# Layer 0's value convolution of images 1 to 7: from halves once to halves twice, with tokens still on partitions

## The chip, the cores and the metric

The kernel runs on one core of a Trainium2 chip. The metric is the device time of one execution in microseconds (us); lower is better. Every time of one engine's work below comes from a single execution recorded by the hardware profiler.

## The reference, cut to what matters

Eight images of 512 channels and 32 x 32 = 1024 tokens, all in float32, pass through two attention blocks. A 1x1 convolution is a matrix product of a 512 x 512 weight with the 512 x 1024 image.

```python
# layer 0: 8 heads of 64 channels, 32 norm groups
h = group_norm(x)                                  # over groups of 16 channels
q, k, v = split(w_qkv @ h + b_qkv)                 # three 512 x 512 products
weight = softmax((q * s)^T (k * s))                # per head, 1024 x 1024
a = v weight^T                                     # per head
x = x + w_proj @ a + b_proj

# layer 1: one head of 512 channels, 8 norm groups
xn = group_norm(x); q, k, v = q_w xn + q_b, k_w xn + k_b, v_w xn + v_b
x = x + p_w @ (softmax(q^T k / sqrt(512)) v) + p_b
```

## The kernel before, in words

**Products by halves.** The 512-wide products are done with the seven-product scheme of Strassen and Winograd. In a "once halved" product (`by_token`, `by_channel`, `values1`) both factors are cut in halves in both directions and seven products of half the size replace eight. In a "twice halved" product (`conv2`, line 498) each of the seven products is cut again in the same way, so 49 products of 128 x 128 weights replace 64. What such a product needs ahead of TensorE's work: sums of quarters of the weight, made once in the prologue and kept in DRAM (`keep` at line 290 for once halved, `keep2` at 296 for twice halved, which computes four further sums on GpSimd at line 306); sums of halves of the normed image, the *image factors* `t_h` (`image_factors`, on VectorE); and for twice halved products the *inner factors* `inner_h` (`inner_factors`, 28 subtractions on GpSimd at line 411 for an image). The sums of the results run on the engines that empty PSUM: VectorE and ScalarE, and GpSimd at line 532 for a few.

**Which product has which form, before.** Layer 0's v and layer 1's z (the folded value and projection weights) are once halved with tokens on partitions: the image is the stationary factor and the weights move, 256 columns at a time. Layer 0's k and q and layer 1's g (image times m, the folded key and query weights) are twice halved with channels on partitions: the weights are stationary, the image moves, 256 columns at a time. The projection p is once halved, channels on partitions. In `conv2` a pair of outer products runs seven steps j; `ps` has a 256-column half for each of the pair's products:

```python
def mm(ps, j, start):
    for i, p in enumerate(products):
        matmul(ps[:, i, :], w[:, i, j - 1, :], f[p][j], start=..., stop=True, skip_group_check=True)
```

Every matmul of the program appears as two records in the trace, on TensorE's matmul row (PE) as on its weight-load row (PEld). All of them come from one helper, line 67, so groups are told apart by the names of their tiles: `psa_v`, `psb_v` and `psc_v` are the PSUM tiles of v, and so on.

**Order of the work.** The first image's v, q and k are made in the prologue, once halved. Then for each image b the main loop does: layer 0's attention of image b (`attention0`); its projection with the residual, and a store to DRAM (`projection`, line 927); layer 1 of image b - 1 (g, scores, z, and the weighted sum `values1`, whose tiles are called `av`, with the output's stores at line 750); then v, k and q of image b + 1 (`values`, `keys_and_queries`). Image 0 has no layer 1 before it, so it goes from attention to v of image 1, then to its own projection, then k and q. One period of the loop, from image to image, is about 348 us.

**Queues.** TensorE's order is that of the program. A product's last two steps (3 and 4 of its last pair) are deferred and run behind step 1 of the next product, so that TensorE has work while PSUM is emptied. Work of the other engines is hung in as *hooks* after a given step, or as a `background` list of which a step takes one or more entries; the image factors, the inner factors and the norm statistics of the next image are such entries. VectorE, ScalarE, GpSimd and SyncE, which issues the DMAs, each take their queue in order; a scheduler orders what isn't pinned with `tc.keep_in_program_order`.

**Buffers.** Images and factors live in a rotating pool of 32 tiles of 128 x 1024 elements (`big_tile`). Weights come from DRAM in the order of the list `uses` into a pool of three buffers of 1792 KB (`wpool`, tag "w"); `load_weight` (lines 325 and 328) issues the next load of that list when a product has taken its weights. The norm statistics of image b + 1 are made from a load of their own, called `ahead`, during v of image b; the image itself is loaded again, as `h`, when it is normed, in the weighted sum of layer 1 (`begun`, line 209).

Of the kernel before, what the change touches and what calls it, by code (L numbers as in the profile page):

```python
# [9 lines left out]
F32 = mybir.dt.float32  # L10
# [19 lines left out]
def two_attention_blocks_kernel(  # L30
# [145 lines left out]
    def main_path(ctx):  # L176
# [114 lines left out]
            nc.sync.dma_start(wdram[n], t)  # L291


        wdram2 = {n: dram.tile([P, 7, 7, P], F32, name=f"sums2_{n}") for n in "qkm"}

        def keep2(n, t):

            u = wpool.tile([P, 4, 7, P], F32, tag="w", name=f"prepare2_{n}")
            quarter = lambda k, i: t[:, :, k, ts(i, P)]
            a11, a21, a12, a22 = quarter(0, 0), quarter(0, 1), quarter(1, 0), quarter(1, 1)  # L300
            s1, s2, s3, s4 = (u[:, i, :, :] for i in range(4))
            for dst, x, y, op in (
                (s1, a21, a22, ALU.add), (s2, s1, a11, ALU.subtract), (s3, a11, a21, ALU.subtract),
                (s4, a12, s2, ALU.subtract),
            ):
                tc.keep_in_program_order(nc.gpsimd.tensor_tensor(dst, x, y, op))
            for j, f in enumerate((a11, a12, s4, a22, s1, s2, s3)):
                nc.sync.dma_start(wdram2[n][:, :, j, :], f)

        twice = {n: [(n, 0), (n, 1)] for n in wdram2}  # L310
        uses = ["v", "p", *twice["k"], *twice["q"]] if B > 1 else ["p"]
        for b in range(1, B):
            uses += ["p", *twice["m"], "z"] + (["v", *twice["k"], *twice["q"]] if b + 1 < B else [])
        uses += [*twice["m"], "z"]
        loaded = []

# [178 lines left out]
            tail.extend([lambda: step(3), lambda: step(4)])  # L495
            tail.extend(final)

        def conv2(n, f, bias, name, hooks=(), after=()):

            out = channel_tiles(name)
            hooks = list(hooks)

            def blocks(places, r, cc):

                if len(places) == 2 and places[0][0] == places[1][0] and places[0][1] < places[1][1]:
                    t = out[2 * places[0][0] + r].rearrange("p (c q n) -> p c q n", c=2, q=2)  # L510
                    return [t[:, :, cc, :]]
                return [
                    out[2 * i + r].rearrange("p (c q n) -> p c q n", c=2, q=2)[:, c : c + 1, cc, :] for i, c in places
                ]

            def add(dst, ps, x):

                n = max(len(dst), len(x))
                for i in range(n):
                    d = dst[i] if len(dst) == n else dst[0][:, i : i + 1, :]  # L520
                    psi = ps[:, i : i + 1, :] if n > 1 else ps
                    xi = x[i] if len(x) == n else x[0][:, i : i + 1, :]
                    if isinstance(d, tuple):
                        d, oc = d
                        nc.vector.scalar_tensor_tensor(d, psi, bias[:, oc : oc + 1], xi, ALU.add, ALU.add)
                    else:
                        nc.vector.tensor_add(d, psi, xi)  # L527

            def more(dst, x, y, r, cc):

                (d,), (x,), (y,) = (blocks([at], r, cc) for at in (dst, x, y))
                nc.gpsimd.tensor_tensor(d, x, y, ALU.add)  # L532

            def biased_half(i, c):
                if bias is not None:
                    for r in range(2):
                        oc = 2 * i + r
                        t = out[oc][:, ts(c, HT)]
                        tc.keep_in_program_order(nc.scalar.activation(t, t, AF.Identity, bias=bias[:, oc : oc + 1]))

            def pair(s, products, y, x, final):
                def written(r, cc):
                    to = blocks(y, r, cc)
                    if s < 3 or bias is None:
                        return to
                    return [(t, 2 * i + r) for t, (i, _) in zip(to, y)]

                w = weights2[s // 2][:, (0, 2, 0, 1)[s] :]

                def mm(ps, j, start):  # L550
                    for i, p in enumerate(products):
                        matmul(ps[:, i, :], w[:, i, j - 1, :], f[p][j], start=start and i == 0, stop=True, skip_group_check=True)

                def extra(r, cc, read, done):
                    if products == (7,):
                        if read:
                            more((0, 1), (0, 1), (1, 1), r, cc)
                        if done:
                            more((1, 1), (1, 0), (1, 1), r, cc)

                inner_steps(
                    f"{name}_{s}", s % 2, len(products), mm, add, written, x and (lambda *at: blocks(x, *at)),
                    extra, hooks.pop(0) if hooks else (), final,
                )

            weights2 = [weight_part((n, 0))]
            pair(0, (1, 5), [(1, 0), (1, 1)], None, [])
            pair(1, (2, 6), [(0, 0), (0, 1)], [(1, 0), (1, 0)], [load_weight, lambda: biased_half(0, 0)])
            weights2.append(weight_part((n, 1)))
            pair(2, (7,), [(1, 0)], [(0, 1)], [lambda: biased_half(1, 1)])  # L570
            pair(3, (3, 4), [(0, 1), (1, 0)], [(0, 1), (1, 0)], [load_weight, *after])
            return out
# [31 lines left out]
        def attention0(b, q, k, v, a, extra):  # L604
            n = 0

            for hp in range(KC):
                for tb in (0, 1) if hp < KC - 1 else (1, 0):
# [22 lines left out]
                    for s in range(NS):  # L631
                        for j in range(2):
                            matmul(
                                av[ts(j, 64), :], v[s // 2][:, s % 2, hp * P + j * 64 : hp * P + (j + 1) * 64],
                                es[s][:, j, :], start=(s == 0), stop=(s == NS - 1),
                            )
                    for f in extra.pop(0) if extra else ():
# [175 lines left out]
        def prologue():  # L813
# [26 lines left out]
            v = by_token(weight_factors(first["v"][0]), hf, "v0_0", middle=(2, 5, 6, 7), back=4)  # L840
            finish()
            run_background(len(background))
            keep("v", first["v"][0])
            x1 = [load_x(1, c, "x1") for c in range(KC)] if B > 1 else []
            norm1 = GroupNorm(0, "0_1")
            background.extend(lambda c=c: norm1.stats(c, x1[c]) for c in range(len(x1)))
# [21 lines left out]
                lambda: tc.keep_in_program_order(nc.vector.tensor_add(obias[0], bias[2], pcols("bp0"))),  # L868
                load_weight,
            ])  # L870
            return v, q, k, norm1, later

        psum_pools("first", 2)
        v, q, k, norm0, later = prologue()
# [11 lines left out]
        def begun(load, norm, b, what):  # L886
# [3 lines left out]
            def start(c):  # L890
# [3 lines left out]
                t, [lambda c=c: start(c) for c in range(KC)],  # L894
                [lambda c=c: norm.apply(nc.scalar, t[c], t[c], c) for c in range(KC)],
            )

        def projection(b, af, xt, hooks=()):

# [39 lines left out]
                [lambda: norm.affine(acc_tile(f"gvar_{uid}")[:, :KC])],  # L939
            ]  # L940

        def values(b, hf, hooks=()):

            inner, steps = inner_factors(hf, f"h0_{b}")
            background.extend(steps)
            norm = None
            if b + 1 < B:
                norm = GroupNorm(0, f"0_{b + 1}")
                for c in range(KC):
                    background.append(lambda c=c: norm.stats(c, load_x(b + 1, c, "ahead")))  # L950
            v = by_token(weight("v"), hf, f"v0_{b}", middle=(2, 5, 6, 7), hooks=hooks, back=4, after=[load_weight])
            return v, inner, norm

        def keys_and_queries(b, f, norm, hooks):

# [45 lines left out]
        for b in range(B):  # L1001
# [21 lines left out]
                    extra[2 * i + 3] += fs  # L1023
            elif B > 1:
                hf, t = image_factors(h, "h0_1", here)
                for i, fs in enumerate((t[:2], (t[2], t[4]), (t[6], t[3]), (t[5], t[7]))):
                    extra[2 * i + 7] += fs
            psum_pools(f"attention_{b}", 1)
            scaled = attention0(b, q, k, v, a, extra)
            if b > 0:  # L1030
                for f in steps[4:7]:
                    f()
            psum_pools(f"products_{b}", 2)
            xt = [load_x(b, c, "x") for c in range(KC)]
            if b > 0:

                inner, sums2 = inner_factors(hf, f"h1_{b - 1}", tc.keep_in_program_order)
                for f in sums2:
                    f()
                norm1, stats = projection(b, af, xt, [scaled, steps[7]])  # L1040
                gf, gsteps = layer1_scores(b - 1, inner)
                _, _, mean, affine = norm_hooks(norm1, f"1_{b}")
                if b + 1 < B:
                    h, loads, applies = begun(load_x, norm0, b + 1, "h0")
                else:
                    h, loads, applies = begun(load_again, norm1, b, "h1")
                ahead = [loads, *([f] for f in applies)]
                layer1_rest(b - 1, inner, gf, gsteps, stats, [[], mean, [], affine], ahead)
                if b + 1 < B:
                    hf, steps = image_factors(h, f"h0_{b + 1}")  # L1050
                    background.extend(steps)
                    v, f, norm0 = values(b + 1, hf)
                    q, k = keys_and_queries(b + 1, f, norm0, ())
            elif B > 1:
                v, f, norm0 = values(1, hf, [[], [], [], [], [*steps[:7], scaled, steps[7]]])
                norm1, stats = projection(0, af, xt)
                hooks = norm_hooks(norm1, "1_0")
                hooks[0].append(lambda: background.extend(stats))
                q, k = keys_and_queries(1, f, norm0, hooks)
            else:  # L1060
                for f in (*steps[:7], scaled, steps[7]):
                    f()
# [211 lines left out]
```

## Time and profile before

| what | value |
|---|---|
| median of 3 runs | 2842.77 us (2842.6 to 2843.14) |
| span of the profiled execution | 2841.1 us |
| what lies around the span, from the median | 1.7 us |
| TensorE busy, and its granted clock | 99%, full speed |
| VectorE, GpSimd, ScalarE busy | 73%, 42%, 33% |
| DMA | 280.6 MB, 98 GB/s |
| records on TensorE's matmul row | 11,846 |

The span runs from the first instruction to the last, and the metric is a little longer. The busy shares are averages over stages of a different kind, so each stage is read by itself. The stages that the change touches lie as follows for image 2, in us from the span's start: the weighted sum `av` of layer 1 from 554.96, its last steps ending at 613.5; v with its first step at 596.3 and the rest from 613.5 to 635; k to 656.9; q to 677.8; layer 0's attention to 795. In image 0's case, attention ends at 237.6, v of image 1 runs to 265.4, the projection to 286.6, and k and q to 330.2.

```profile
core 0: us, PE busy (x) PEld busy (x) DVE busy (x) ACT busy (x) POOL busy (x), PEclk, DMA share, GB/s
554.50:613.50 59.00, 59.00 (x169) 30.61 (x169) 41.23 (x51) 7.28 (x8) 33.60 (x36) 1.00 0.35 132
613.50:635.00 21.50, 21.50 (x101) 18.84 (x100) 13.03 (x24) 1.74 (x3) 0.00 (x0) 1.00 0.35 119
635.00:656.90 21.90, 21.90 (x104) 18.90 (x103) 12.69 (x34) 4.41 (x8) 7.03 (x11) 1.00 0.42 148
656.90:677.80 20.90, 20.84 (x95) 17.52 (x94) 12.83 (x31) 6.67 (x11) 5.88 (x10) 1.00 0.73 277
677.80:795.00 117.20, 117.20 (x574) 42.91 (x576) 98.71 (x85) 68.13 (x76) 20.55 (x14) 1.00 0.13 46
```

Each row is a stretch of time with the busy time of each engine in it and the number of its records; DVE is VectorE, ACT ScalarE, POOL GpSimd, PE TensorE.

### The profile page before, as it was taken

The numbers are of one execution on the slowest core, as the hardware profiler recorded it, in microseconds if no ns is written. First come the engines' busy times: TensorE is split into PE (matmuls) and PEld (weight loads), VectorE is DVE, ScalarE is ACT, GpSimd is POOL, SyncE is SP. The second block draws the span as 40 slices with busy tenths as digits, with TensorE's granted clock in tenths as the row PEclk, the third lists the DMA queues.
The fourth block names the chain that finished last, engine by engine and source line by source line (L and its number), as shares of the span: only waits on it lengthen the run. The fifth ranks groups of instructions, "written<-read, shape, count | busy, mean of one in ns | idle before, by whom it ended". The sixth has DMA issues, their size and how long they took to land.

```text
span 2841.1 us, 32477 instructions
## 1 busy us (share of the span) xinstructions
PE 2824.5 (99%) x11846; PEld 1689.7 (59%) x11846; DVE 2082.5 (73%) x2733; ACT 928.1 (33%) x1177; POOL 1201.3 (42%) x1193
## 2 busy tenths in 40 slices
PE   9999999999999999999999999999999999999999
PEld 5435635866367653677537774376743868338584
DVE  5587787766877678776787757877578775887765
ACT  1252452214522145220552215422154311633130
POOL 2123215732167321673217721277123771147672
PEclk9999999999999999999999999999999999999999
DMA  8632403133041230322313232132321323112301
GB/s 280 195 119 90 180 20 126 35 144 137 20 145 62 110 128 22 139 94 98 109 49 112 94 109 101 49 108 94 138 72 49 108 101 135 42 45 102 119 4 68
DMA packets 91597, 280.59 MB, mean 99 GB/s; under 512 B 10595, under 2 KB 36387, under 8 KB 82470
## 3 DMA queue, kind: packets, MB, share of 16 engines
q1 hardware_dynamic: 89638, 276.15, 27.1%
q10 hardware_dynamic: 1792, 2.29, 0.2%
q8 instruction: 96, 1.57, 0.2%
q14 instruction: 71, 0.58, 0.1%
HBM read 227.31 MB, written 51.09 MB: 98 GB/s over the span
## 4 chain that ended last, share of the span: by engine, by line
PE 97%; DVE 2%; issue 1%; POOL 0%; ACT 0%; DVEq 0%; POOLq 0%; ACTq 0%
PE sc L67 16%; PE av L67 16%; PE psb_av L67 6%; PE psb L67 5%; PE psa_av L67 4%; PE psc_av L67 4%; PE psc L67 3%; PE psa L67 3%; PE psb_z L67 3%; PE psb_p L67 3%; PE psb_v L67 3%; PE psb_k L67 3%; PE psb_g L67 3%; PE psb_q L67 2%; PE psa_p L67 2%; PE psa_z L67 2%
## 5 line engine op out<-in xcount | busy, mean ns | idle before, releaser
L626 DVE TENSOR_TENSOR sum<-sum,e 128x1024 f32<-128x1024 f32 x384 | 522.7, 1361 | 41.4 <-DVE sum L624 0.9
L622 ACT ACTIVATE e<-sc 128x1024 f32<-128x1024 f32 x512 | 476.1, 1054 | 79.5 <-PE sc L67 79.5
L67 PE MATMUL sc<-q,k 64*128 64x512 f32 x2048 | 456.8, 596 | 0.0
L67 PE MATMUL av<-e,v 128*64 128x512 f32 x2048 | 453.6, 596 | 0.0
L67 PEld LDWEIGHTS sc<-q,k 64*128 64x128 f32 x2048 | 191.8, 186 | 238.3 <-ACT e L622 109.1
L67 PEld LDWEIGHTS av<-e,v 128*64 128x64 f32 x2048 | 141.4, 137 | 304.3 <-issue 304.3
L588 POOL TENSOR_TENSOR all_recs<-all_recs,rc 128x256 f32<-128x256 f32 x72 | 65.2, 906 | 529.8 <-DVE rc L586 522.2
L645 POOL TENSOR_TENSOR a<-a,r 128x512 f32<-128x512 f32 x56 | 109.7, 1959 | 270.6 <-DMA r<-rows 250.2
L586 DVE RECIPROCAL rc<-sums 128x256 f32<-128x256 f32 x72 | 126.5, 1757 | 45.8 <-PE sums L67 25.9
L532 POOL TENSOR_TENSOR k<-k,k 128x256 f32<-128x256 f32 x28 | 20.1, 726 | 315.6 <-DVE u_k L527 315.6
L640 ACT COPY a<-av 128x512 f32<-128x512 f32 x64 | 37.4, 585 | 317.4 <-PE av L67 317.4
L624 DVE TENSOR_TENSOR sum<-e,e 128x1024 f32<-128x1024 f32 x64 | 78.5, 1226 | 57.3 <-ACT e L622 57.3
L67 PE MATMUL psb<-inner,inner_h 128*128 128x256 f32 x448 | 116.1, 382 | 1.2 <-DVE u L672 0.5
L67 PE MATMUL psa_av<-e,z 128*128 128x512 f32 x256 | 113.3, 596 | 0.0
L411 POOL TENSOR_TENSOR inner_h<-h,inner_h 128x256 f32<-128x256 f32 x120 | 108.7, 908 | 2.2
L140 ACT ACTIVATE h<-h,b,s 128x1024 f32<-128x1024 f32 x62 | 78.3, 1268 | 92.8 <-DMA h<-in_x 75.3
L67 PEld LDWEIGHTS psb<-inner,inner_h 128*128 128x128 f32 x448 | 84.0, 190 | 16.8 <-POOL inner L426 3.8
L411 POOL TENSOR_TENSOR inner_h<-h 128x256 f32<-128x256 f32 x60 | 58.9, 982 | 77.8 <-ACT h L140 66.6
L686 POOL TENSOR_TENSOR sum<-sum,e 128x1024 f32<-128x1024 f32 x32 | 76.1, 2378 | 27.3 <-ACT e L682 26.1
L67 PE MATMUL psb_g<-inner_h,w_m 128*128 128x256 f32 x336 | 86.0, 383 | 0.3
L411 POOL TENSOR_TENSOR inner_h<-t_h 128x256 f32<-128x256 f32 x90 | 79.2, 883 | 12.7 <-PE psc_av L67 9.5
L67 PEld LDWEIGHTS psa_av<-e,z 128*128 128x128 f32 x256 | 48.1, 190 | 57.2 <-issue 56.5
(344 smaller groups left out, 5529.9 us busy)
## 6 DMA issues: line engine op xcount, KB each, us to landing
x<-in_x SPq DMA_DIRECT2D x36, 512.0 KB
h<-in_x SPq DMA_DIRECT2D x32, 512.0 KB
spill<-x SPq DMA_DIRECT2D x32, 512.0 KB
h<-spill SPq DMA_DIRECT2D x32, 512.0 KB
x<-spill SPq DMA_DIRECT2D x32, 512.0 KB
out<-x SPq DMA_DIRECT2D x64, 256.0 KB
w_p<-sums_p SPq DMA_DIRECT2D x8, 1792.0 KB
r<-rows SPq DMA_DIRECT2D x112, 128.0 KB
```

The costliest lines, as they stand in the source:

```text
L67: tc.keep_in_program_order(nc.tensor.matmul(*args, **kw))
L140: tc.keep_in_program_order(nc.scalar.activation(dst, src, AF.Identity, bias=b, scale=s))
L411: pin(nc.gpsimd.tensor_tensor(dst, x, y, ALU.subtract))
L532: nc.gpsimd.tensor_tensor(d, x, y, ALU.add)
L586: nc.vector.reciprocal(rc, sums)
L588: nc.gpsimd.tensor_tensor(all_recs, all_recs, rc, ALU.add)
L622: nc.scalar.activation(e, sc, AF.Exp, scale=(C // 8) ** -0.5)
L624: nc.vector.tensor_add(total, es[0], e)
L626: nc.vector.tensor_add(total, total, e)
L640: nc.scalar.copy(dst, av)
L645: nc.gpsimd.tensor_tensor(dst, dst, r, ALU.mult)
L686: on = lambda dst, x, y: lambda: tc.keep_in_program_order(nc.gpsimd.tensor_tensor(dst, x, y, ALU.add))
```

## The change

Layer 0's v of images 1 to 7 becomes twice halved (`conv2` with a new switch `by_tokens`), with tokens still on partitions. The inner factors that k and q already need serve v too, as its stationary factor: each 256-token factor gives two stationary slices of 128 x 128, and the 128 columns of a weight quarter move. An image's v has 98 matmuls with 128 moving columns, where it had 56 with 256. The result lies in another layout, and attention reads v through a function `v(s, head)`.

What follows from it in the program: the sums of v's weights are made by `keep2`, whose four sums now lie in four tiles of the big pool in place of one weight buffer; v's weights are two loads (1792 and 1344 KB) and stand behind p's in `uses`. The inner factors, and the image factors from which they are made, must be there before v's second step, so they are begun in hooks of the layer 1 weighted sum (`factors_ahead`) and no longer in v's background. The statistics of the next image stay in the background list of `values`, but are now the first in it; since v's first step runs ahead of the last steps of the weighted sum, their loads and their eight operations now stand among the weighted sum's stores and evacuations on SyncE and VectorE. Image 0's projection now stands ahead of v of image 1, as in the other images, and the inner factors of image 1 are made ahead of it. VectorE gets 20 more operations for an image, ScalarE 4, GpSimd 8.

```diff
-        wdram2 = {n: dram.tile([P, 7, 7, P], F32, name=f"sums2_{n}") for n in "qkm"}
+        wdram2 = {n: dram.tile([P, 7, 7, P], F32, name=f"sums2_{n}") for n in "qkmv"}
 
         def keep2(n, t):
 
-            u = wpool.tile([P, 4, 7, P], F32, tag="w", name=f"prepare2_{n}")
+            u = [big_tile(f"prepare2_{n}_{i}", (P, 7, P)) for i in range(4)]
...
-        uses = ["v", "p", *twice["k"], *twice["q"]] if B > 1 else ["p"]
+        layer0 = [*twice["v"], *twice["k"], *twice["q"]]
+        uses = ["p", *layer0] if B > 1 else ["p"]
         for b in range(1, B):
-            uses += ["p", *twice["m"], "z"] + (["v", *twice["k"], *twice["q"]] if b + 1 < B else [])
+            uses += ["p", *twice["m"], "z"] + (layer0 if b + 1 < B else [])
...
                 def mm(ps, j, start):
                     for i, p in enumerate(products):
-                        matmul(ps[:, i, :], w[:, i, j - 1, :], f[p][j], start=start and i == 0, stop=True, skip_group_check=True)
+                        wt = w[:, i, j - 1, :]
+                        if not by_tokens:
+                            matmul(ps[:, i, :], wt, f[p][j], start=start and i == 0, stop=True, skip_group_check=True)
+                            continue
+                        for h in range(2):
+                            matmul(
+                                ps[:, i, ts(h, P)], f[p][j][:, ts(h, P)], wt,
+                                start=start and (i, h) == (0, 0), stop=True, skip_group_check=True,
+                            )
...
-                                av[ts(j, 64), :], v[s // 2][:, s % 2, hp * P + j * 64 : hp * P + (j + 1) * 64],
+                                av[ts(j, 64), :], v(s, 2 * hp + j),
...
-            keep("v", first["v"][0])
+            keep2("v", first["v"][0])
...
+        def factors_ahead(h, loads, applies, uid):
+
+            made, hooks = {}, [[] for _ in range(5)]
+
+            def begin():
+                for f in loads:
+                    f()
+                hf, t = image_factors(h, uid)
+                made["inner"], inner = inner_factors(hf, uid)
+                hooks[1] += applies[:1]
+                hooks[2] += [applies[1], inner[0], *t[:2]]
+                hooks[3] += [*applies[2:], inner[1], *t[2:4]]
+                hooks[4] += [*inner[2:4], lambda: background.extend([*t[4:6], *inner[4:6], *t[6:], inner[6]])]
+
+            hooks[0].append(begin)
+            return hooks, made
...
-        def values(b, hf, hooks=()):
-
-            inner, steps = inner_factors(hf, f"h0_{b}")
-            background.extend(steps)
+        def values(b, f, hooks=()):
+
             norm = None
             if b + 1 < B:
                 norm = GroupNorm(0, f"0_{b + 1}")
                 for c in range(KC):
                     background.append(lambda c=c: norm.stats(c, load_x(b + 1, c, "ahead")))
-            v = by_token(weight("v"), hf, f"v0_{b}", middle=(2, 5, 6, 7), hooks=hooks, back=4, after=[load_weight])
-            return v, inner, norm
+            v = conv2("v", f, None, f"v0_{b}", hooks, by_tokens=True)
+            return lambda s, head: v[head // 2][:, s * P + head % 2 * 64 : s * P + head % 2 * 64 + 64], norm
...
                 hf, t = image_factors(h, "h0_1", here)
-                for i, fs in enumerate((t[:2], (t[2], t[4]), (t[6], t[3]), (t[5], t[7]))):
+                for i, fs in enumerate((t[:2], (t[2], t[4]), (t[6], t[3]), (t[5], t[7], *steps[:2]), steps[2:4])):
                     extra[2 * i + 7] += fs
...
-            if b > 0:
+            if B > 1:
                 for f in steps[4:7]:
                     f()
             psum_pools(f"products_{b}", 2)
             xt = [load_x(b, c, "x") for c in range(KC)]
-            if b > 0:
-
-                inner, sums2 = inner_factors(hf, f"h1_{b - 1}", tc.keep_in_program_order)
+            if B > 1:
+
+                inner, sums2 = inner_factors(hf, f"h1_{b - 1}" if b > 0 else "h0_1", tc.keep_in_program_order)
                 for f in sums2:
                     f()
                 norm1, stats = projection(b, af, xt, [scaled, steps[7]])
+            if b > 0:
...
                 if b + 1 < B:
                     h, loads, applies = begun(load_x, norm0, b + 1, "h0")
+                    ahead, made = factors_ahead(h, loads, applies, f"h0_{b + 1}")
...
-                    hf, steps = image_factors(h, f"h0_{b + 1}")
-                    background.extend(steps)
-                    v, f, norm0 = values(b + 1, hf)
-                    q, k = keys_and_queries(b + 1, f, norm0, ())
+                    v, norm0 = values(b + 1, made["inner"])
+                    q, k = keys_and_queries(b + 1, made["inner"], norm0, ())
             elif B > 1:
-                v, f, norm0 = values(1, hf, [[], [], [], [], [*steps[:7], scaled, steps[7]]])
-                norm1, stats = projection(0, af, xt)
+                v, norm0 = values(1, inner)
...
-                q, k = keys_and_queries(1, f, norm0, hooks)
+                q, k = keys_and_queries(1, inner, norm0, hooks)
```

More of the change, by code (lines that the diff above doesn't have):

```diff
@@ L291, in keep @@
             nc.sync.dma_start(wdram[n], t)
-        wdram2 = {n: dram.tile([P, 7, 7, P], F32, name=f"sums2_{n}") for n in "qkm"}
+        wdram2 = {n: dram.tile([P, 7, 7, P], F32, name=f"sums2_{n}") for n in "qkmv"}
         def keep2(n, t):
-            u = wpool.tile([P, 4, 7, P], F32, tag="w", name=f"prepare2_{n}")
+            u = [big_tile(f"prepare2_{n}_{i}", (P, 7, P)) for i in range(4)]
             quarter = lambda k, i: t[:, :, k, ts(i, P)]
             a11, a21, a12, a22 = quarter(0, 0), quarter(0, 1), quarter(1, 0), quarter(1, 1)
-            s1, s2, s3, s4 = (u[:, i, :, :] for i in range(4))
+            s1, s2, s3, s4 = u
             for dst, x, y, op in (
@@ L496, in inner_steps, with conv2 @@
             tail.extend(final)
-        def conv2(n, f, bias, name, hooks=(), after=()):
+        def conv2(n, f, bias, name, hooks=(), after=(), by_tokens=False):
             out = channel_tiles(name)
@@ L870, in prologue @@
             ])
-            return v, q, k, norm1, later
+            return lambda s, head: v[s // 2][:, s % 2, ts(head, 64)], q, k, norm1, later
         psum_pools("first", 2)
@@ L1044, in main_path @@
                     h, loads, applies = begun(load_x, norm0, b + 1, "h0")
+                    ahead, made = factors_ahead(h, loads, applies, f"h0_{b + 1}")
                 else:
                     h, loads, applies = begun(load_again, norm1, b, "h1")
-                ahead = [loads, *([f] for f in applies)]
+                    ahead = [loads, *([f] for f in applies)]
                 layer1_rest(b - 1, inner, gf, gsteps, stats, [[], mean, [], affine], ahead)
                 if b + 1 < B:
-                    hf, steps = image_factors(h, f"h0_{b + 1}")
-                    background.extend(steps)
-                    v, f, norm0 = values(b + 1, hf)
-                    q, k = keys_and_queries(b + 1, f, norm0, ())
+                    v, norm0 = values(b + 1, made["inner"])
+                    q, k = keys_and_queries(b + 1, made["inner"], norm0, ())
             elif B > 1:
-                v, f, norm0 = values(1, hf, [[], [], [], [], [*steps[:7], scaled, steps[7]]])
-                norm1, stats = projection(0, af, xt)
+                v, norm0 = values(1, inner)
                 hooks = norm_hooks(norm1, "1_0")
                 hooks[0].append(lambda: background.extend(stats))
-                q, k = keys_and_queries(1, f, norm0, hooks)
+                q, k = keys_and_queries(1, inner, norm0, hooks)
             else:
```

## The prediction

> **What bounds the kernel now.** I read the page's engine totals first, then the chain that ended last, then the waits of TensorE:
>
> ```profile
> PE 2824.5 (99%) x11846; PEld 1689.7 (59%) x11846; DVE 2082.5 (73%) x2733; ACT 928.1 (33%) x1177; POOL 1201.3 (42%) x1193
> PE 97%; DVE 2%; issue 1%; POOL 0%; ACT 0%; DVEq 0%; POOLq 0%; ACTq 0%
> PE tr_wk L70 <- DMA rawk<-in_w: 3.7, 1, 3.7
> PE psa_v L67 <- POOL h L142: 0.8, 1, 0.8
> PE psb_v L67 <- DVE w_v L238: 0.5, 1, 0.5
> ```
>
> TensorE is busy 99% of 2841.1 us and makes 97% of the chain; apart from the first load (3.7 us) no wait of it exceeds 0.8 us. So TensorE's stream is the time: what shortens it counts in full, as long as no other engine comes late. All the others have room (VectorE, the busiest, 73%). Next I read the groups of the two convolutions that matter, v as it is, and k, which already runs in the form that v is to take:
>
> ```profile
> L67 PE MATMUL psb_v<-w_v,t_h 128*128 128x256 f32 x224 | 50.9, 381 | 0.0
> L67 PE MATMUL psa_v<-w_v,h 128*128 128x256 f32 x224 | 50.6, 380 | 0.0
> L67 PE MATMUL psb_k<-inner_h,w_k 128*128 128x256 f32 x294 | 75.4, 384 | 0.0
> ```
>
> The mean of 380 ns is no price: records overlap. 224 records busy for 50.9 us are 227 ns each, and from start to start I find 216 ns for 256 moving columns. Each matmul of the program leaves two records. The five v groups of images 1 to 7 have 784 records, 112 an image, and take 24.2 us an image from start to start. k has 98 an image and takes 21.6: 98 x 0.216 = 21.2, and 0.45 more lost at its narrow steps.
>
> The change halves the moving columns of v to 128, and the page has no such stream with these weights. Two places come near. The transposes of the value weights move 128 columns; the small statistics products load the same 128x128 weights as v but move 4:
>
> ```profile
> 100.11 1.40 PEld L70 LDWEIGHTS tr_wv<-ident,rawv 128*128 128x128 f32 x13 [0.75 <-DVE k L387]
> 101.48 0.30 PEld L67 LDWEIGHTS gmean<-mv,gm 128*128 128x128 f32 x2
> L67 PEld LDWEIGHTS psb_v<-w_v,t_h 128*128 128x128 f32 x224 | 42.2, 190 | 7.0 <-DVE w_v L238 1.1 <-issue 0.5
> ```
>
> Thirteen transposes start 1.40 - 0.14 = 1.26 us apart from first to last; in the run of them after the first pair, each starts 109 ns after the one before. Two weight loads of 190 ns each end within 0.30 us, so the second starts 0.11 us after the first: the load's 190 ns is a latency, and loads follow each other every 110 to 112 ns.
>
> [...] the next load starts 2 ns after a matmul starts, and a 256-column record costs 216 ns, not 216 + 110. [...]
>
> **The change part by part.** The sum is made against the profiled execution (2841.1); the median, 2842.77, lies 1.7 above, and I carry that.
>
> *v on TensorE.* Per image 56 matmuls x 2 records x 256 columns become 98 x 2 x 128: 12.5% fewer columns. Bounds of the pitch: 109 ns (transposes) and 190 (the load's duration, if it could not overlap). I take 111, what the loads alone show: 196 x 0.111 = 21.76, and I add k's 0.45 for narrow steps: 22.2 us. 22.2 - 24.2 = -2.0 us, times 7 = **-14.0 us**; at 109 ns it is -16.7. Break-even is (24.2 - 0.45)/196 = 121 ns.
>
> *v's evacuations.* VectorE goes from 10 operations of 0.69 us to 26 of 0.42 (k's 256-column row, 421 ns) and 4 of 0.69: 13.7 us an image, +6.8. ScalarE goes from 4 copies to 8 of about 0.57, GpSimd gets 8 sums of 0.726 (k's row), 5.8 us. v's stage (613.5 to 635.0 us for image 2) has VectorE busy 13.0 of 21.5, of which 5.3 are the eight norm statistics of the next image that move out, GpSimd 0 and ScalarE 1.7. So 14.5 of 22 us: k carries the same work now at 12.7 of 21.9 and costs the 0.45 that I have counted. Nothing more.
>
> *Norm statistics of the next-but-one image, moved ahead.* The four loads and eight statistics leave v for the steps of the second attention's weighted sum (L750's stores stand in this queue). Before, SyncE issued the loads behind all eight output stores:
>
> ```profile
> 574.46 41.80 SPq L750 DMA_DIRECT2D out<-x  x8
> 616.36 1.82 SPq L209 DMA_DIRECT2D ahead<-in_x  x4
> L98 DVE BATCH_NORM_STATS2 bnst<-ahead 128x6 f32<-128x512 f32 x48 | 29.9, 665 | 22.8 <-DMA ahead<-in_x 22.8
> ```
>
> Now they stand among the stores, and on VectorE the statistics stand in front of the evacuation w_av of that stage's first pair. Issue is possible at about 589.5 us of this trace (the buffer comes free with a matmul of step 6); with the 4.0 us that the load took here (616.36 to 620.39), w_av is done at 594.9, and TensorE wants it at 597.2. VectorE itself goes from 41.2 to 46.5 of 59 us there. Cost nothing, with 2.3 us of cover; what lies past it is a rival below.
>
> *Inner factors of the next image* (28 GpSimd operations, some 25 us) were done before k, at 575.9 to 603.1; v needs them from its second step, about 611. 8 us of cover: nothing.
>
> *Weight loads.* v's one load of 1792 KB becomes 1792 + 1344 KB, seven more DMAs, and each later load moves one place in the list. The next is issued 10 us or more before its use: nothing. DMA engines are busy a third of these stages.
>
> *Prologue and image 0, once.* Preparing v's sums takes four GpSimd operations of 2.085 us (row of q's) in a gap of that engine from 26.0 to 51.3 us: hidden. Seven stores of 448 KB replace one of 1792 and stand on SyncE ahead of image 1's loads, which land some 4 us later with 5 to 7 of slack before their statistics stand in the way of q's evacuation. Later loads shift too: the raw projection weights come behind the stores of m's sums, at 109 to 113 us instead of 80, and a bias product wants them at 116.3: 0 to 2 us. Image 0's projection moves ahead of image 1's v: its 8 spill and residual steps keep their order, the transition from attention to projection costs 0.3 us in image 1 (447.39 to 447.70), as attention to v did here (237.55 to 237.85); its four x loads and the scale's row loads pass with some 11 us to spare. Between -1 and +3, I take **+1**.
>
> Sum: -14.0 + 1 = -13: 2828.1 against the span, **2829.8** as median.
>
> **Rivals.** (1) *The weight load doesn't fit beside a 128-column record.* [...] at 190 ns +95: 2938. It ends slower from 125 ns on. For it: the load's 190 ns[...]. Against it: 110 ns in both neighbours. (2) *The moved statistics come in front of a needed evacuation.* If the load takes over 6.4 us from issue (h<-in_x, behind four other loads, took 8.9 at 565.7), TensorE waits; at 8.9 it is 2.5 us for each of five or six images, 12 to 15 us, which eats the gain: 2842. For it: stores and loads share the queue there. Against: one load heads the four. (3) *Evacuation paces v* as k's last pair is paced, at 1 to 1.5 us an image in place of 0.45: 2834 to 2837. (4) That nothing changes on TensorE is excluded: 98 matmuls of half width are in the new program.
>
> **How the numbers follow.** A measurement here can tell about 0.2%, 5.7 us: faster means below 2837.1, slower above 2848.5. Forecast (pitch 109 to 115, 2824 to 2834): 0.65. Rival 3: 0.12, all faster but its edge. Rival 2: 0.10, no change. Rival 1: 0.13, slower. The range, 2822 to 2842, holds the first three cases and leaves out rival 1 and a few in a hundred at either end. Faster 0.76, same 0.11, slower 0.13.
>
> **What would show it.** v's three groups with 128 moving columns: 1372 records busy for 150 to 156 us, so 109 to 114 ns each. Waits of TensorE on w_av or bnst<-ahead near zero; over 1 us an image is rival 2. Waits of psb_v on the copies and on k-like sums: rival 3. ps_bias waiting on a DMA: the prologue's cost. The prediction is wrong where v's busy time over its records exceeds 121 ns, or where the second attention's weighted sum gets longer.

## The result, and the profile after

The changed kernel takes 2846.38 us (median of 12 runs, 2843.84 to 2847.37); beside it the kernel before took 2843.85 (12 runs, 2842.60 to 2845.68). The ratio is 1.0006, 95% interval 0.9998 to 1.0015: no difference that can be told, where 13 us less were forecast. The profiled execution has a span of 2844.5 us, 3.4 more than before.

The engine totals and the chain by engine of the profile after, and the waits of TensorE (us in total, times, longest):

```profile
PE 2817.1 (99%) x12434; PEld 1694.7 (60%) x12434; DVE 2129.8 (75%) x2873; ACT 943.1 (33%) x1205; POOL 1259.7 (44%) x1253
PE 96%; DVE 2%; issue 1%; DMA 0%; ACT 0%; POOL 0%; SPq 0%; DVEq 0%; POOLq 0%; ACTq 0%
PE psb_v L67 <- DVE w_v L238: 4.7, 1, 4.7
PE ps_wz L67 <- issue: 4.5, 1, 4.5
...
PE psb_v L67 <- ACT u_v L450: 1.2, 1, 1.2
...
PE psc_v L67 <- DVE x L934: 0.6, 1, 0.6
```

Two waits above 4 us are new, each once; so are shorter ones, of 1.2, 0.8 and 0.6 us among others. The two long ones are for tiles of the prologue (`w_v` at line 238 belongs to the once halved product, which only image 0 still uses; `ps_wz` is the folding of the value and projection weights). Where the time went shows best in the start of each layer 0 attention, taken from the trace of both kernels:

| attention of image | before, us | after, us | after minus before | gained or lost since the row above |
|---|---|---|---|---|
| 0 (end of the prologue) | 119.82 | 134.56 | +14.7 | +14.7 |
| 1 | 330.46 | 345.22 | +14.8 | 0.0 |
| 2 | 678.11 | 691.10 | +13.0 | -1.8 |
| 3 | 1026.17 | 1036.91 | +10.7 | -2.3 |
| 4 | 1374.21 | 1382.69 | +8.5 | -2.3 |
| 5 | 1721.85 | 1728.50 | +6.7 | -1.8 |
| 6 | 2069.50 | 2074.29 | +4.8 | -1.9 |
| 7 | 2416.65 | 2419.64 | +3.0 | -1.8 |

The row of an attention holds the turn from the attention before it, so v of image 1 is in row 1. Images 2 to 7 gain 11.8 us, 1.96 each: the forecast of 2.0. Image 1's turn gains nothing, and the prologue has lost 14.7 us before the first turn begins. What remains to the end of the span is +0.4.

The largest of v's six new groups on TensorE's matmul row:

```profile
L67 PE MATMUL psb_v<-w_v,inner_h 128*128 128x128 f32 x588 | 77.3, 277 | 1.3 <-ACT u_v L450 1.2
L67 PE MATMUL psa_v<-w_v,h 128*128 128x128 f32 x224 | 34.1, 275 | 0.0
L67 PE MATMUL psc_v<-w_v,inner_h 128*128 128x128 f32 x196 | 26.6, 276 | 0.6 <-DVE x L934 0.6
```

From start to start, v takes 22.2 us in each of images 2 to 7, as forecast, where it took 24.2; in image 1 it takes 25.0, with two waits of 2.1 us together in it. The median distance between two records is 112 ns, forecast 111. The prediction named another sign, the groups' busy time over their records, 109 to 114 ns. By it the three groups above are at 131 to 152 ns (77.3 us over 588 records, 34.1 over 224, 26.6 over 196). That is no longer pitch: the groups now take turns every few records, and each turn ends with a whole record of some 276 ns that overlaps the next group's. By the letter this sign, with its bound of 121 ns, called v wrong where v was right; the distance from start to start isn't touched by the turns.

**The first loss.** VectorE in the profile of before, then of after (start, duration, both in us; x2 and x3 are operations in a row), then GpSimd of after:

```profile
26.46 1.28 DVE L171 TENSOR_TENSOR t_h<-h,t_h 128x512 f32<-128x512 f32 x2
27.66 1.28 DVE L172 TENSOR_TENSOR h<-h,h 128x512 f32<-128x512 f32 x2
41.48 1.89 DVE L286 TENSOR_TENSOR prepare_k<-prepare_k 128x512 f32<-128x512 f32 x3
```

```profile
26.42 5.05 DVE L171 TENSOR_TENSOR t_h<-h,t_h 128x512 f32<-128x512 f32 x2
31.40 5.06 DVE L172 TENSOR_TENSOR h<-h,h 128x512 f32<-128x512 f32 x2
40.11 1.28 DVE L238 TENSOR_TENSOR u_v<-psb_v,t_v 128x512 f32<-128x512 f32 x2
43.07 5.53 DVE L286 TENSOR_TENSOR prepare_k<-prepare_k 128x512 f32<-128x512 f32 x3
48.52 1.28 DVE L238 TENSOR_TENSOR w_v<-psb_v,t_v 128x512 f32<-128x512 f32 x2
```

```profile
25.93 2.50 POOL L306 TENSOR_TENSOR prepare_v<-prepare_v 128x896 f32<-128x896 f32 x1
28.51 2.41 POOL L306 TENSOR_TENSOR prepare_v<-prepare_v,prepare_v 128x896 f32<-128x896 f32 x1
...
42.56 2.41 POOL L306 TENSOR_TENSOR prepare_q<-prepare_q,prepare_q 128x896 f32<-128x896 f32 x1
```

The four VectorE operations at lines 171 and 172 last 2.5 us each, where they took 0.64. Each of them has one GpSimd sum of v's weights beside it and ends about half a microsecond after that sum: the second of line 171 at 31.47, the second sum at 30.92. VectorE comes out 7.5 us later at its sums of q's weights. GpSimd's sums of q follow those at 40.4 us. Before, they started at 51.3, since their buffer was one of the three for weights; in the big pool, with v's sums out of the way, they start at 32.7 (run 3). At 40.4 they meet VectorE's sums of k's weights, which take 5.5 us in place of 1.9. `w_v` starts at 48.5 in place of 43.3, and TensorE waits for it. Between them, `u_v` at 40.11 runs at its usual 0.64 us each beside a GpSimd sum: one of its operands lies in PSUM.

**What a wait costs beyond itself.** Stretches of the profile after, core 0 (length, busy us of the engines with records, granted clock, share of DMA, GB/s):

```profile
44.20:49.20 5.00, 0.36 (x2) 0.00 (x0) 5.00 (x5) 0.00 (x0) 3.25 (x2) 0.89 0.38 119
49.20:54.90 5.70, 5.65 (x13) 4.56 (x14) 2.48 (x4) 0.00 (x0) 0.00 (x0) 0.50 0.84 253
...
114.30:119.60 5.30, 5.28 (x7) 2.20 (x8) 0.52 (x1) 0.00 (x0) 0.00 (x0) 0.50 0.88 266
```

The column behind GpSimd's is the clock that TensorE was granted: 0.50 for more than 5 us after each of the two long waits. Matmuls of 256 columns start 427 ns apart there in place of 216, those of 512 columns 853 in place of 429. So the first loss, 8.0 us in v of image 0, is some 5 us of waiting and 3 of half speed; the second, 6.8 us, is 4.1 and 2.7.

**The second loss.** VectorE ahead of the product for z, after:

```profile
109.90 0.16 DVE L115 COPY gmean<-gmean 128x4 f32<-128x4 f32 x1 [1.85 <-PE gmean L67]
110.09 1.30 DVE L117 TENSOR_TENSOR d<-mv,gmean 128x4 f32<-128x4 f32 x1
111.43 2.00 DVE L119 TENSOR_TENSOR d<-d 128x4 f32<-128x4 f32 x1
113.46 0.16 DVE L121 TENSOR_TENSOR dv<-d,mv 128x4 f32<-128x4 f32 x1
113.54 1.28 DVE L786 COPY natv<-tr_wv 128x512 f32<-128x512 f32 x2
```

The copies of the transposed value weights, `natv`, for which TensorE waits, stood ahead of image 1's group means before and stand behind them now; and two operations on 4 columns last 1.3 and 2.0 us, beside GpSimd's sums of m's weights. Before, the operation at line 119 took 2.0 us there too, but nobody waited for it. The trace puts TensorE's wait down to "issue": it ends at 114.33, when the first of these copies is done.

### The profile page after: what moved, and what is told of

The parts are those of the page before. It is cut to its first block, busy times and chain, and to the rows that moved or that the text cites. A ratio compares the mean times of both kernels' runs of the same rounds, so it can differ in the third digit from the quotient of the medians.

```text
span 2844.5 us, 33986 instructions
## 1 busy us (share of the span) xinstructions
PE 2817.1 (99%) x12434; PEld 1694.7 (60%) x12434; DVE 2129.8 (75%) x2873; ACT 943.1 (33%) x1205; POOL 1259.7 (44%) x1253
## 3 DMA queue, kind: packets, MB, share of 16 engines
q10 hardware_dynamic: 1792, 2.29, 0.2%
## 4 chain that ended last, share of the span: by engine, by line
PE 96%; DVE 2%; issue 1%; DMA 0%; ACT 0%; POOL 0%; SPq 0%; DVEq 0%; POOLq 0%; ACTq 0%
PE sc L67 16%; PE av L67 16%; PE psb_av L67 6%; PE psb L67 5%; PE psa_av L67 4%; PE psc_av L67 4%; PE psc L67 3%; PE psa L67 3%; PE psb_z L67 3%; PE psb_p L67 3%; PE psb_k L67 3%; PE psb_g L67 3%; PE psb_v L67 3%; PE psb_q L67 2%; PE psa_p L67 2%; PE psa_z L67 2%
## 5 line engine op out<-in xcount | busy, mean ns | idle before, releaser
L67 PEld LDWEIGHTS psb<-inner,inner_h 128*128 128x128 f32 x448 | 83.9, 190 | 16.6 <-POOL inner L427 3.5
L412 POOL TENSOR_TENSOR inner_h<-h 128x256 f32<-128x256 f32 x60 | 56.7, 944 | 77.3 <-ACT h L140 77.3
L460 ACT COPY psb_v<-psa_v 128x512 f32<-128x512 f32 (+1 forms) x28 | 14.5, 517 | 223.9 <-DVE o L755 141.6
L533 POOL TENSOR_TENSOR v<-v,v 128x256 f32<-128x256 f32 x28 | 20.1, 727 | 142.7 <-DVE u_v L528 142.7
```

The lines of the kernel that those rows point to most:

```text
L67: tc.keep_in_program_order(nc.tensor.matmul(*args, **kw))
L412: pin(nc.gpsimd.tensor_tensor(dst, x, y, ALU.subtract))
```

## The experiments

All are built from the kernel before or the changed one. Runs 1 to 4 are single executions and are read by their stages. The same stage agrees between executions to some tenths of a microsecond, apart from stretches at half clock, which last longer in some than in others (behind the same wait 6.83 us in the changed kernel and about 3.4 in run 4) and move a stage by about 1 us.

**1. The prologue alone, in the kernel before.**

```diff
-            u = wpool.tile([P, 4, 7, P], F32, tag="w", name=f"prepare2_{n}")
+            u = [big_tile(f"prepare2_{n}_{i}", (P, 7, P)) for i in range(4)]
...
             keep("v", first["v"][0])
+            tv = first["v"][0]
...
+            s1, s2, s3, s4 = [big_tile(f"extra_{i}", (P, 7, P)) for i in range(4)]
...
+                tc.keep_in_program_order(nc.gpsimd.tensor_tensor(dst, x_, y_, op))
```

> The kernel before, with two pieces of the change's prologue and nothing else of it: the four GpSimd sums of v's weights at the change's place (their results are not used), and the buffers of all such sums in the big pool. v of images 1 to 7 stays once halved. Theory A (the loss is in the prologue, and the seven convolutions gain as forecast): about +14 us, 2857 to 2859, with v of image 0 some 8 us longer (32.8 in place of 24.8) and the product for z some 6.8 longer; VectorE's image factors at lines 171 and 172 last about 2.5 us each in place of 0.64 while GpSimd's sums run. Rival B (the loss is from the stores and loads in SyncE's queue that the change adds, or from v's new form in the images): no change against before, 2842 to 2846.

Measured 2859.5 us beside 2843.4: +16.1. Layer 0's first attention starts 16.6 us later, and the span ends 16.6 later. VectorE has the stretched operations, here and at line 172:

```profile
26.50 5.05 DVE L171 TENSOR_TENSOR t_h<-h,t_h 128x512 f32<-128x512 f32 x2
```

The loss needs neither v's new form nor its added loads and stores, which this kernel doesn't have. It is 2 us larger than expected: `w_v` keeps TensorE waiting 6.6 us here, 4.7 in the changed kernel.

**2. Fills in place of the sums.** The buffers as in run 1, and in place of the four sums:

```diff
             keep("v", first["v"][0])
+            for i in range(4):
+                t_ = big_tile(f"extra_{i}")
+                for j in range(2):
+                    tc.keep_in_program_order(nc.gpsimd.memset(t_, 0.0))
```

> As the run before, but the four GpSimd sums of v's weights are eight fills of 128x1024 with zero, which read nothing from SBUF. Theory A1 (a VectorE operation with two SBUF inputs waits while a GpSimd operation that reads SBUF runs): VectorE's lines 171 and 172 at 0.64 us each, v of image 0 as before (24.8 us); the second loss, at the product for z, stays, since the order on VectorE there is that of the change: +6 to +7 us, about 2851. Rival A2 (any GpSimd work beside VectorE, or the write traffic, stretches VectorE's operations): 2 us or more for each of lines 171 and 172, and v of image 0 longer by several us, 2854 or more.

Measured 2850.75, +7.3, as the first theory has it (line 172 is the same):

```profile
26.94 1.28 DVE L171 TENSOR_TENSOR t_h<-h,t_h 128x512 f32<-128x512 f32 x2
```

GpSimd's eight fills, which only write, run from 26.43 to 34.09 us and leave VectorE alone: each operation at lines 171 and 172 takes its 0.64 us beside them. That it takes a GpSimd operation with two inputs is not so either: in the kernel before, the second operation of line 170 in the prologue took 1.52 us in place of 0.74 and ended at 26.54 us, half a microsecond after GpSimd's operation at line 142, whose only large input is one tile of `h`. v of image 0 takes 25.8 us in place of 24.8 (q's sums still meet k's). The wait ahead of the product for z is 4.5 us, so that part doesn't come from v's sums. Run 2 has the fills beside the buffers' change; a program with the buffers' change alone was not run, but it has the four operations on the means ahead of the copies too. What the case shows: beside a GpSimd operation that reads SBUF, these VectorE operations with two SBUF inputs end after it, and the price is 2.5 us for each in place of 0.64. What in the hardware makes it so, no run shows. GpSimd's sums pay too, with 2.4 to 2.5 us in place of the 2.085 that the prediction took.

**3. v's sums after k's, in the changed kernel.**

```diff
-            keep2("v", first["v"][0])
             x1 = [load_x(1, c, "x1") for c in range(KC)] if B > 1 else []
...
             keep2("k", first["k"][0])
+            keep2("v", first["v"][0])
```

> The changed kernel, with the sums of v's weights made after those of q and k. Theory A1: v of image 0 returns to about 24.8 us (at most 26, as q's sums on GpSimd can still meet VectorE's sums of k's weights), no wait for w_v, no half-speed matmuls there: 8 us less, about 2838. The wait ahead of the product for z stays. Rival (the late w_v comes from the loads, not from GpSimd): v of image 0 still 30 us or more, 2845.

Measured 2837.5: 8.9 less than the changed kernel's median. v of image 0 takes 25.1 us, `w_v` starts at 43.40, no half-speed stretch follows it; the wait for `natv` stays at 4.5.

**4. The copies ahead of the means, in the changed kernel.**

```diff
-            nc.vector.tensor_copy(self.gmean, ps)
+            pin = tc.keep_in_program_order if self.uid == "0_1" else lambda ins: ins
+            pin(nc.vector.tensor_copy(self.gmean, ps))
...
-            nc.vector.tensor_sub(d, mean, self.gmean)
+            pin(nc.vector.tensor_sub(d, mean, self.gmean))
...
```

> The changed kernel, with the four small VectorE operations on image 1's group means pinned to the order of the program, behind the two copies of the transposed value weights. Theory C (those four stand ahead of the copies in VectorE's queue, two of them held up by GpSimd's sums of m's weights, and TensorE waits for the copies 4.5 us and then runs at half speed for some 5 us): the wait ahead of the product for z goes and the product takes 13.4 us as before: 6 to 7 us less, about 2839.5. v of image 0 stays at 32.8. Rival D (TensorE waits there for the raw weights or another load): no change, the wait stays at 4 us or more, with another releaser.

Measured 2838.3, 8.1 less than the changed kernel's median (7.5 by the start of the first attention, 1.1 of them in v of image 0, whose stretch at half speed was shorter in this execution); the product for z takes 13.4 us again and nothing waits for a load there. VectorE in that kernel:

```profile
108.50 1.29 DVE L787 COPY natv<-tr_wv 128x512 f32<-128x512 f32 x2 [1.40 <-PE tr_wv L70]
...
110.50 2.00 DVE L120 TENSOR_TENSOR d<-d 128x4 f32<-128x4 f32 x1
```

The four-column operation still takes its 2.0 us, behind the copies.

**5. Both remedies.** The edits of 3 and 4 together.

> The changed kernel with both edits at once: v's sums after k's, and the mean chain behind the copies. If the two losses are separate, they add: 2846.4 - 8.9 - 6.5 = 2831, which is 12 us less than before; seven images at -2.0 give -14, and image 0 keeps a loss of 2. If removing one only uncovers the other (a common later wait, such as the raw projection weights that the bias product needs), it stays at 2836 to 2838.

Measured 2833.6 us (5 runs, 2831.8 to 2834.1) beside 2843.1: ratio 0.9964, interval 0.9951 to 0.9978. The prologue ends at 120.3 us, 0.5 later than before, so the losses add. It is 2.6 short of what was expected, and the profile shows 1.6 of it: image 1's turn is that much longer than before. The same two waits as in the changed kernel, 2.1 us within 3 us, are followed by a stretch at half clock, which the changed kernel's profile didn't have at that place:

```profile
264.00:268.00 4.00, 2.19 (x16) 1.81 (x15) 4.00 (x9) 1.66 (x3) 0.44 (x1) 0.97 1.05 353
268.00:271.00 3.00, 3.00 (x16) 3.00 (x15) 1.78 (x4) 0.00 (x0) 0.00 (x0) 0.50 1.01 301
```

**6. Image 2's statistics held back to k.**

```diff
-                    background.append(lambda c=c: norm.stats(c, load_x(b + 1, c, "ahead")))
+                    (held if b == 1 else background).append(lambda c=c: norm.stats(c, load_x(b + 1, c, "ahead")))
...
-                hooks[0].append(lambda: background.extend(stats))
+                hooks[0].append(lambda: background.extend([*stats, *held]))
```

> The run before with one more edit: for image 1's v alone, the loads and statistics of image 2 are held back until k, behind those of image 0's residual. Theory: the 1.2 us that TensorE waits for ScalarE's copy u_v and the 0.6 us for VectorE's residual in image 1's v come from these statistics standing ahead of the residual; without them 2 us less, 2829, and image 1 gains 2 us against before like the others. Rival: the backlog comes from the residual's sums being held up by GpSimd's inner factors, which lie there now: no gain, 2831.

Measured 2833.4 (2832.9 to 2834.2), no gain over run 5. Neither text had it right: the waits do leave v, but only for k:

```profile
PE psc_k L67 <- DVE c_k L529: 1.3, 1, 1.3
PE psb_k L67 <- DVE k L529: 0.9, 1, 0.9
```

**7. The same statistics in layer 0's attention of image 1.** As run 6, but `held` is hung into that attention, the mean chain into the z product of layer 1, and the statistics of image 0's residual are pinned behind all of the residual.

> The kernel with both prologue remedies, with the statistics of image 2 (loads, eight operations, and their mean chain) moved out of image 1's v and k into layer 0's attention of image 1 and the z product after it, and the statistics of image 0's residual pinned to program order, so that all of the residual stands ahead of them on VectorE. Theory (VectorE has too much before it at image 1's v and k, and any of it that stays there only moves the wait): both waits go, no half-speed stretch in image 1's v, image 1 gains 2 us like the others: 2829 to 2830, 13 to 14 us less than before. Rival (the residual's sums wait for GpSimd's inner factors, so the backlog stays): 2832 to 2834, with psc_v waiting for the residual as before.

Measured 2836.3 (9 runs, 2835.2 to 2837.6), 2.7 us more than run 5. Image 1's turn does gain 1.5 us, but the mean chain, now in z, keeps TensorE waiting for the accumulator tile of the sums, again with half speed behind it (the next stretch, 557.4 to 562.0 us, has a granted clock of 0.65):

```profile
PE sums L67 <- DVE ve L127: 2.5, 1, 2.5
```

**8. The mean chain in the projection and g.** As run 7, with that chain two products earlier.

> The run before with the mean chain of image 2's statistics moved from the z product of layer 1 into the projection and the g product of image 1's turn. Theory (the 2.9 us that TensorE waited for the sums in that run, with five matmuls at half speed behind it, came from that chain standing on VectorE and in the shared accumulator tile there; image 1's own turn is cured): 2830 to 2832, with image 1 about 1.5 us less than before and image 2's turn at -2 like the others. Rival (the statistics in layer 0's attention cost it time themselves): 2834 or more, with a wait on the sums in the attention of image 1.

Measured 2832.3 (5 runs, 2831.2 to 2833.5): ratio 0.9960, interval 0.9946 to 0.9974. The wait for `sums` in z is gone (2.5 us by the view of waits, where the text on record has 2.9), image 1's turn gains 1.5 us and image 2's products 2.0. But layer 0's attention of image 1 is 1.0 us longer, waiting twice about half a microsecond for `sums` where there was no wait, as the rival had it, and the projection and g behind it are 0.2 longer each. So both were half right. Runs 5, 6 and 8 can't be told apart by their times; all three are faster than the kernel before, measured beside them, by 0.3 to 0.4%.

## Why the prediction was wrong

**Right: v on TensorE.** In six of seven images, 22.2 us for the 22.2 forecast, 112 ns for 111, and 1.96 us gained for 2.0. The weight load does fit beside a 128-column record: with 112 ns from one record to the next, its duration is still 192 ns in the mean, as a latency. Rival 1, a load that doesn't fit, did not come; the 109 to 112 ns of the neighbours were a better price than the load's 190. Rival 3, evacuation that paces v, did not come either, outside image 1.

**Nearly right: the moved statistics.** Cover of 2.3 us was forecast and all of it was used up: in five images one distance between records of `psb_av` is 566 to 582 ns in place of 429 and the next is 504 (before, this was so in one image), about 0.2 us an image. Rival 2 had the right place, at 0.2 us in place of 2.5.

**Wrong: "Preparing v's sums takes four GpSimd operations ... in a gap of that engine ...: hidden".** This is the step that failed. The gap was read on GpSimd's own row and never against what VectorE did in it, and a cost was put at nothing that was half of the loss. The term "Prologue and image 0, once", taken at +1 with bounds of -1 and +3, measured +14.7 for the prologue (8.0 in v of image 0 by this step, 6.8 ahead of and in the product for z by the next one), and image 1 did not get its 2 us. Run 1 makes that loss without the rest of the change, run 2 takes v's part of it away by taking the reads away, and run 3 by moving the sums. The prediction counted the four sums at their own 2.085 us and no operation of VectorE as longer. The price stood in the profile of before:

```profile
L171 DVE TENSOR_TENSOR t_h<-h,t_h 128x512 f32<-128x512 f32 x16 | 17.7, 1142 | 0.0
L1017 DVE TENSOR_TENSOR h<-h,h 128x512 f32<-128x512 f32 x16 | 11.0, 686 | 0.0
L119 DVE TENSOR_TENSOR d<-d 128x4 f32<-128x4 f32 x16 | 19.4, 1211 | 0.5
```

Lines 171 and 1017 do the same kind of operation on as many columns. At line 1017 GpSimd is idle each time; at line 171 it makes inner factors beside 14 of the 16, and those last 1.21 us, the other two 0.68 (two such records in a row overlap and take 1.28). Line 119, on 4 columns, lasts 0.16 us in the eight cases where GpSimd is idle and 2.0 to 2.3 us in the other eight. A mean that differs so much between two equal operations, or is so long for 4 columns, is the sign to look for.

**Wrong in the same term: the order on VectorE.** The working listed the loads and stores that pass each other in SyncE's queue, but not that the scheduler had turned round the means and the copies for z on VectorE, which can be seen in the program's order before any run. Run 4 shows it to be worth 6.8 us, and runs 2 and 3, which have it without the first loss, 5.7 to 5.8 with a shorter stretch at half clock. The waits that were listed (the raw projection weights at the bias product, image 1's loads at q) did not show.

**Missing: half speed after a wait.** The working counted a wait as its length. Each wait of TensorE of 2.5 us or more in these traces, apart from the first load, was followed by matmuls at half clock, and in the changed kernel that made up 5.7 of the 14.8 us that the two waits cost. Added up from the granted clock, the stretches at half clock lasted 6.83 us for each of the changed kernel's two waits and about 6.8 for each of run 1's (6.6 and 4.5 us), and about 3.4 in runs 2 to 5, one each; behind the 2.5 us of run 7 it was 3.2 us or more. The length of the wait doesn't settle it: the same wait of 4.7 us for `w_v` was followed by 6.83 us of half clock in the changed kernel and by about 3.4 in run 4, and the same 2.1 us of waits in image 1 by about 3.4 us in run 5 and by none in the changed kernel. What does settle it was not shown.

**Image 1.** Why it gained nothing is settled in part. Its v takes 25.0 us where that of the other images takes 22.2: its two waits are 2.1 us, smaller ones 0.7. That is even 0.8 more than the 24.3 of before. The table has 0.0 and not +0.8 because layer 0's attention of image 0 became 0.8 us shorter, as it did in run 1, where v has its old form. Runs 6 to 8 show that moving the statistics out of v takes the two waits away, and that VectorE's work for image 2 cost time wherever it was put next: waits of 1.3 and 0.9 us in k, 2.5 us and a stretch at half clock in z, 1.5 us in attention, projection and g together. Whether some place holds it free of cost stays open; a run without these eight operations was not made.

## What to carry to other kernels

An engine's idle time is not free room: before work is put on GpSimd, look at what VectorE does in the same microseconds, and whether both read SBUF (here 2.5 us in place of 0.64 for an operation). Where a gain is spread over a loop (here seven times 2 us), look as hard at the one-time part, since a single wait of 4 to 5 us cost 7 to 8 with the slow clock behind it. After any change of buffers, compare the order on each queue before and after: an order that nobody pinned can turn round, and here that was 6.8 us.

## What the runs showed of the hardware that was not expected

- In the changed kernel's prologue, a VectorE operation with both operands in SBUF ended only after the GpSimd sum that ran beside it: 2.5 us in place of 0.64 for 512 columns, 2.0 us in place of 0.16 for 4 columns. One with an operand in PSUM (0.64 us) was not held up, and neither was anything beside GpSimd's fills in run 2 (0.64 us an operation).
- After waits of 2.5 to 6.6 us, apart from that for the first load, TensorE ran at half clock: for 6.83 us twice in the changed kernel, about 6.8 twice in run 1, about 3.4 once in each of runs 2 to 4, 3.2 or more in run 7. After one of 1.5 us (run 2) it did not.
